# Finishing a quad's last group beside two softmax stages, and splitting the last quad's division over three engines

## The chip, the cores and the metric

The program runs on one core of one Trainium2 chip. The metric is the device time of one execution in microseconds; for the kernel before it is 2020.35 us, the median of three runs (2018.48 to 2020.65). One further execution was profiled and traced. All times of single instructions are from that trace and count from the start of its span.

## What is computed

A graph attention layer with a residual, over 12,500 nodes of 128 features and 200,000 edges that are sorted by their destination:

```python
h = relu(layernorm(x))
hn = (h @ W_node.T).reshape(nodes, 4, 32)
e  = (edge_attr @ W_edge.T).reshape(edges, 4, 32)
att = sum(concat([hn[src], hn[dst], e]) * a, -1)          # one logit per edge and head
att = where(att > 0, att, 0.2 * att)
m   = maximum(segment_max(att, dst), 0)
ex  = exp(att - m[dst])
deg = segment_sum(1, dst)
denom = segment_sum(ex, dst) + (num_edges - deg) * exp(-m)
out = x + segment_sum(ex / denom[dst] * hn[src], dst)
```

The division can wait until the sums are complete, since `denom` belongs to the destination.

## The kernel before

**Tiling.** The edges are cut into 392 *groups* of 511 (and one row that carries a sum over from the group before). Four groups make a *quad*; there are 98 quads, numbered 0 to 97 (`nq` is 98). Two to four quads make a *super*, for which the softmax is done in one go: 28 of them, numbered 0 to 27. Super 2 (the third) holds quads 4 to 7, super 27 (the last) quads 96 and 97. Destinations of a group fit a window of 92 rows.

**The steps of a quad.** `fetch` loads edge features (`ea`), destinations (`db`) and two sets of windows (`pw`, `xw`) through the queue of SyncE (SP), and gathers the source rows from a table in DRAM into `ga`, by sixteen indirect DMAs that GpSimd (POOL) issues one after the other (line 141). `ga` is a ring of eight quads, so a group's gather has to wait until the group 32 places earlier has had its last matmul, line 686. `all_logits` makes the logits: VectorE (DVE) marks the destinations (line 534, which needs `db`), TensorE (PE) multiplies (lines 540, 543), DVE adds the pieces and the gathered part (lines 555, 557). `softmax(s)` turns the logits of a super and scans along the edges; it is one long chain that goes to and fro between DVE, PE and ScalarE (ACT), in five steps separated by `yield` (lines 583 to 592; 595 to 606; 609 to 619; 624 to 641; 644 to 659). `sums(q)` handles the four groups of a quad: DVE weights the gathered rows (line 734) and marks the slots (738), PE multiplies three of four tiles into `acc` (743).

**Completing and dividing.** The first row of a group carries the sum of the group before. So the fourth matmul pair of a group (686) is issued late, by `complete()`, after the next group's first three: DVE scales the carried row (681), ACT copies its count (685), PE multiplies (686), ACT copies `acc` to `pt` (687) and, where a piece of the quad is complete, computes `exp(-m)` into `den` (694). The piece is a whole quad; in quads 95, 96 and 97 it is three, two and one group. The next call of `complete()` divides the piece: six DVE instructions (lines 755, 757, 760, 761, 765, 769), of which the last, adding `x`, is on POOL for quad 96 and for the last group of quad 95. Then SP writes each group's 92 rows (line 772). Windows of neighbouring groups overlap, so each write waits for the one before it.

**Order.** The order of issue on every engine is written out by hand. `together` takes one step of each of its generators in turn. A stage `s` runs the last quad of the super before (`sums(q0 - 1)`), the logits of one quad of the next super and `softmax(s)` side by side. In stage 2 three groups of quad 3, and in stage 27 two groups of quad 95, are issued before that. In both the last group is left incomplete, and its completion and the division come inside the next quad's `sums`, when the softmax is done. In the last two quads the marks of line 738 come from POOL instead (line 711, after the last gather). A few matmuls without use (`run_on`, line 573) keep PE occupied in the last softmax.

Of the kernel before, what the change touches and what calls it, by code (L numbers as in the profile page):

```python
# [8 lines left out]
F32 = mybir.dt.float32  # L9
BF16 = mybir.dt.bfloat16  # L10
I32 = mybir.dt.int32
AF = mybir.ActivationFunctionType
OP = mybir.AluOpType
AX = mybir.AxisListType

P = 128
H, HD = 4, 32
# [7 lines left out]
R_CNT, R_SRC, ROW = H * HW, H * HW + 1, H * HW + 5  # L25
# [5 lines left out]
SPAN = 92  # L31
QG = 4
# [11 lines left out]
def blocks(total, step):  # L44
    return [(i, min(step, total - i)) for i in range(0, total, step)]
# [3 lines left out]
def kernel(  # L49
# [35 lines left out]
    nc = tc.nc  # L85
# [5 lines left out]
    consts = ctx.enter_context(tc.tile_pool(name="consts", bufs=1))  # L91
# [9 lines left out]
    part = consts.tile([P, 1], F32, name="part")  # L101
# [2 lines left out]
    lane = consts.tile([P, WIN], F32, name="lane")  # L104
    nc.gpsimd.iota(lane, pattern=[[1, WIN]], base=0, channel_multiplier=0,
                   allow_small_or_imprecise_dtypes=True)
    ones = consts.tile([P, P], F32, name="ones")
    nc.vector.memset(ones, 1.0)

# [12 lines left out]
    quads = blocks(G, QG)  # L122
    nq = len(quads)
# [21 lines left out]
    def held_gather(q, i, rows, width):  # L145

        nc.vector.memset(ga_all[0:1, q % QUADS, i, 0, 0:1], 0.0)
        gather(q, rows, width, i, i + 1)

    def together(*steps):  # L150
        steps = list(steps)
        while steps:
            steps = [st for st in steps if next(st, steps) is not steps]
# [3 lines left out]
    with tc.manual_schedule():  # L157
# [6 lines left out]
        for _ in range(AT_ONCE):  # L164
            q, i = early.pop(0)
# [12 lines left out]
        with tc.tile_pool(name="prep", bufs=1) as prep, tc.tile_pool(  # L178
            name="prep_ps", bufs=1, space=bass.MemoryType.PSUM
# [127 lines left out]
        with tc.tile_pool(name="node", bufs=2) as node, tc.tile_pool(  # L307
            name="node_ps", bufs=2, space=bass.MemoryType.PSUM
        ) as node_ps, tc.tile_pool(name="index", bufs=1) as index, tc.tile_pool(
            name="index_ps", bufs=1, space=bass.MemoryType.PSUM  # L310
# [111 lines left out]
            step, steps = 0, sum(-(-T // 3) for T in sizes) - 9  # L422
# [40 lines left out]
    with tc.tile_pool(name="work", bufs=2) as work, \  # L463
# [20 lines left out]
        def windows(of, size, g, n):  # L484

            return nc.values_load_multi_w_load_instructions(  # L486
                of[0:1, g:g + n], engines=[mybir.EngineType.SP], min_val=0, max_val=(N - 1) * size,
                skip_runtime_bounds_check_because="a destination's row, and that is a node")[1]
# [16 lines left out]
        def fetch(q):  # L505
            if q not in EA:
                fetch_edges(q)
            fetch_windows(q)
            if q not in GATHERED:
                GATHERED.add(q)  # L510
                gather(q, table, ROW, raws(q), quads[q][1])
# [156 lines left out]
        def complete():  # L668

            division = state.pop("division", None)  # L670
            if begun:
                complete_group(*begun.pop())
            if division:
                divide(*division)

        def complete_group(q, i, ga, hot, pt, acc, fc):
            g0, m = quads[q]
            g = g0 + i
            if g:
                before = state["before"]  # L680
                nc.vector.tensor_tensor(  # L681
                    ga[0:1, i, 0, 0:H * HW].rearrange("p (h w) -> p h w", w=HW),
                    before[WIN:WIN + 1, 0:H * HW].rearrange("p (h w) -> p h w", w=HW),
                    fc.unsqueeze(2).to_broadcast([1, H, HW]), op=OP.mult)
                nc.scalar.copy(ga[0:1, i, 0, R_CNT:R_CNT + 1], before[WIN:WIN + 1, R_CNT:R_CNT + 1])  # L685
            nc.tensor.matmul(acc, hot[:, i, 0, :], ga[:, i, 0, :], start=False, stop=True)  # L686
            nc.scalar.copy(pt[:, i, :], acc)  # L687
            state["before"] = acc

            part = {nq - 1: 1, nq - 2: 2, nq - 3: 3}.get(q, QG)  # L690
            if (i + 1) % part == 0 or i == m - 1:
                lo = i - i % part
                den = work.tile([SPAN, QG, H], F32, name="den")
                nc.scalar.activation(den[:, lo:i + 1, :], pt[0:SPAN, lo:i + 1, R_SRC:R_SRC + H],
                                     AF.Exp, scale=-1.0)
                state["division"] = q, pt, den, lo, i + 1


# [49 lines left out]
        def divide(q, pt, den, lo, hi):  # L748

            n = hi - lo  # L750
            xw = XW[q][:, lo:hi]
            pt = pt[0:SPAN, lo:hi]
            den = den[:, lo:hi]
            others = work.tile([SPAN, QG], F32, name="others")
            nc.vector.tensor_scalar(others[:, :n], pt[:, :, R_CNT], -1.0, float(E),
                                    op0=OP.mult, op1=OP.add)
            nc.vector.tensor_tensor(den, den, others[:, :n].unsqueeze(2).to_broadcast([SPAN, n, H]),
                                    op=OP.mult)
            val = pt[:, :, 0:H * HW].rearrange("p g (h w) -> p g h w", w=HW)
            nc.vector.tensor_tensor(den, den, val[:, :, :, HD], op=OP.add)  # L760
            nc.vector.reciprocal(share_ps[:, :n, :], den)
            if not lo:
                RES[q] = work.tile([SPAN, QG, D], F32, name="res")
            res = RES[q][:, lo:hi]
            nc.vector.tensor_tensor(  # L765
                res[:, :n, :].rearrange("p g (h d) -> p g h d", d=HD), val[:, :, :, 0:HD],
                share_ps[:, :n, :].unsqueeze(3).to_broadcast([SPAN, n, H, HD]), op=OP.mult)
            add = nc.gpsimd if q == nq - 2 or q == nq - 3 and lo else nc.vector
            add.tensor_tensor(res[:, :n, :], res[:, :n, :], xw, op=OP.add)  # L769
            at = windows(base_row, 4 * D, quads[q][0] + lo, n)  # L770
            for i in range(n):
                nc.sync.dma_start(rows_at(out, at[i], 4 * D), as_bytes(res[:, i, :]))
# [14 lines left out]
        def late(q, copy=nc.scalar.copy):  # L787

            return [converted(q, acc_pool, work, copy)]

        def normed(q):
            return several(2, raw_statistics(raw_pool, q), raw_scaled(q))
# [39 lines left out]
        with tc.manual_schedule():  # L832
            for q in range(min(2, nq)):
                fetch(q)
            on_vector = nc.vector.tensor_copy
            assert supers[0] == (0, 2) and supers[1] == (2, 2)

            held = [(q, i) for q in range(raw, min(QUADS, nq)) for i in range(raws(q), quads[q][1])]
            GATHERED.update(range(raw, QUADS))

            def some(*numbers):
                for n in numbers:
                    for _ in range(min(n, len(held))):
                        held_gather(*held.pop(0), table, ROW)
                    yield

            together(some(2, 0, 1, 0, 1), *late(0, on_vector), normed(1))
            together(some(1, 0, 1, 0, 1), *late(1, on_vector), all_logits(0), normed(2))
            together(some(0, 0, 1), all_logits(1), raw_statistics(raw_pool, 3))
            check_steps = checked()  # L850
            for s, (q0, m) in enumerate(supers):


                ahead = list(range(q0 + m, sum(supers[s + 1]))) if s + 1 < len(supers) else []
                now, ahead = ahead[:1], ahead[1:]
                beside = [sums(q0 - 1)] if s else late(2) + [raw_scaled(3)]
                beside += late(raw) if s == 1 else []
                if s in (2, len(supers) - 1):

                    for _ in range(3 if s == 2 else 2):  # L860
                        next(beside[0])
                if not s:
                    beside.insert(0, some(1, 1, 1, 1, 1, len(held)))
                together(*beside, *map(all_logits, now), softmax(s))
                assert not held
                for k in range(m - 1):
                    now, ahead = ahead[:1], ahead[1:]
                    together(sums(q0 + k), *map(all_logits, now), *([] if s else [normed(raw)]))
                    if s > 4:
                        next(check_steps, None)  # L870
                for a in ahead:
                    together(all_logits(a))
                if not s:
                    complete()
                    together(*late(3))
            flush()
            together(check_steps)
            last_sums = sums(nq - 1)
            next(last_sums)
            redo = nc.values_load(flag[0:1, 0:1], min_val=0, max_val=1)  # L880
            together(last_sums)
            complete()
            complete()
# [197 lines left out]
```

## Time and profile before

| | us |
|---|---|
| median of three runs | 2020.35 |
| the profiled execution, its own time | 2020.54 |
| its span, first to last instruction | 2018.7 |
| PE matmul busy | 1376.0 (68%) |
| DVE busy | 1367.8 (68%) |
| ACT busy | 405.9 (20%) |
| POOL busy | 1507.4 (75%) |
| gathers from the table, line 141: 1494 of 949 ns | 1418.3 |
| granted TensorE clock, mean | 0.541 |

Busy shares are means over the whole span. A line of the timeline gives the start, the duration, the engine, the line of the kernel, the operation with its tiles and shapes, how many instructions were merged, and in brackets how long the engine had been idle and what released it. For a DMA queue the duration is that of issuing, with the waits in between.

### The profile page before, as it was taken

To read this page: it belongs to the slowest core of one execution; us is meant where nothing else is said; L and a number is where in the kernel's file an instruction comes from. 1 tells how busy PE (TensorE), PEld (TensorE's weight loads), DVE (VectorE), ACT (ScalarE), POOL (GpSimd) and SP (SyncE) were. 2 spreads that over 40 slices of the span, in tenths; PEclk is the share of its full clock that TensorE was granted. 3 is DMA by queue.
4 is the path that set the end of the run, shared out by engine and by line. 5 is a ranking of instruction groups with operands and counts; after the bars stand their busy time and mean duration, and the time that the engine had idled before them with its cause. 6 is when DMAs were issued, how large, how long until landed. Compare 5 with 4: busy or idle time off the path is not lost.

```text
span 2018.7 us, 27303 instructions
## 1 busy us (share of the span) xinstructions
PE 1376.0 (68%) x7317; PEld 1249.1 (62%) x7317; DVE 1367.8 (68%) x3368; ACT 405.9 (20%) x1532; POOL 1507.4 (75%) x1609
## 2 busy tenths in 40 slices
PE   6687777767767766666757666667566666777776
PEld 4576666667666655656656565556565565666665
DVE  7676766767776765666757656666567576768876
ACT  6664111111111111111111111111111111112112
POOL 7777677777777777777777777777777777777774
PEclk8767555555555555555555555555555555556556
DMA  7665665666656665655555565556555655565640
GB/s 250 211 164 126 156 164 136 157 156 157 151 145 167 154 148 145 157 140 147 146 138 152 134 152 133 151 141 146 137 150 131 155 141 141 135 157 129 155 106 25
DMA packets 195661, 297.23 MB, mean 147 GB/s; under 512 B 70441, under 2 KB 143337, under 8 KB 186098
## 3 DMA queue, kind: packets, MB, share of 16 engines
q1 hardware_dynamic: 143696, 183.27, 34.3%
q0 software_dynamic: 50112, 109.61, 23.3%
q10 hardware_dynamic: 1698, 2.58, 0.4%
q8 instruction: 61, 1.00, 0.2%
q14 instruction: 94, 0.77, 0.1%
HBM read 269.61 MB, written 25.71 MB: 146 GB/s over the span
## 4 chain that ended last, share of the span: by engine, by line
DMA 31%; DVE 22%; PE 16%; POOL 13%; issue 10%; SPq 4%; ACT 4%; DVEq 0%; ACTq 0%; POOLq 0%
POOL ga L141 13%; DMA out_dram<-res 10%; DMA ga<-table,srci 10%; DMA db<-in_dst_dram 9%; PE acc L743 6%; DVE at L534 4%; PE lg L543 3%; DMA pw<-side 2%; DVE ga L734 2%; DVE hot L738 2%; DVE res L765 2%; DVE res L769 2%; PE acc L686 2%; DVE ga L681 1%; SPq L486 1%
## 5 line engine op out<-in xcount | busy, mean ns | idle before, releaser
L141 POOL DMA_INDIRECT ga<-table,srci x1494 | 1418.3, 949 | 460.5 <-issue 394.7
L743 PE MATMUL acc<-ga,hot 128*97 128x137 f32 x2352 | 644.8, 445 | 63.0 <-DVE hot L738 31.0
L743 PEld LDWEIGHTS acc<-ga,hot 128*97 128x97 f32 x2352 | 515.6, 278 | 85.7 <-DVE hot L738 36.9
L540 PEld LDWEIGHTS <-at 92*128 92x128 bf16 x1568 | 214.5, 165 | 506.4 <-DVE at L534 488.0
L540 PE MATMUL lg<-pw,at 92*128 92x12 bf16 x1568 | 169.3, 181 | 435.3 <-DVE at L534 427.3
L543 PE MATMUL lg<-wblk,ea 128*128 128x8 f32 x1568 | 406.8, 357 | 0.0
L543 PEld LDWEIGHTS lg<-wblk,ea 128*128 128x128 f32 x1568 | 379.4, 307 | 0.0
L534 DVE TENSOR_TENSOR at<-const_ps,db 92x512 bf16<-92x512 f32 x392 | 266.9, 682 | 7.7 <-DMA db<-in_dst_dram 1.7
L734 DVE TENSOR_TENSOR ga<-ga,ex_ps 128x528 f32<-128x528 f32 x392 | 268.5, 685 | 0.4
L686 PE MATMUL acc<-ga,hot 128*97 128x137 f32 x784 | 257.2, 431 | 1.3 <-ACT ga L685 1.0
L687 ACT COPY pt<-acc 97x137 f32<-97x137 f32 x392 | 107.4, 274 | 721.9 <-PE acc L686 721.9
L557 DVE TENSOR_TENSOR U<-st,ga 128x64 f32<-128x64 f32 x98 | 26.5, 270 | 308.6 <-DMA ga<-table,srci 300.4
L738 DVE TENSOR_TENSOR hot<-const_ps,slot 128x384 f32<-128x384 f32 x384 | 208.8, 544 | 0.0
L686 PEld LDWEIGHTS acc<-ga,hot 128*97 128x97 f32 x784 | 198.5, 282 | 2.8 <-ACT ga L685 2.8
L681 DVE TENSOR_TENSOR ga<-acc,facs 1x132 f32<-1x132 f32 x391 | 115.7, 296 | 115.0 <-ACT pt L687 107.3
L685 ACT COPY ga<-acc 1x1 f32<-1x1 f32 x391 | 59.9, 153 | 483.0 <-DVE ga L681 476.1
L765 DVE TENSOR_TENSOR res<-pt,const_ps 92x512 f32<-92x512 f32 (+2 forms) x103 | 67.7, 657 | 82.2 <-DMA out_dram<-res 79.0
L141 POOL DMA_INDIRECT ga<-in_x_dram,srci x72 | 69.4, 964 | 23.2 <-issue 18.0
L769 DVE TENSOR_TENSOR res<-res,xw 92x512 f32<-92x512 f32 (+1 forms) x100 | 67.5, 675 | 3.5
L395 PE MATMUL row_ps<-wcat,hT 128*128 128x137 f32 x198 | 39.3, 348 | 21.0 <-DVE tgt L401 11.0
L555 DVE TENSOR_REDUCE st<-lg 128x64 f32<-128x192 f32 x98 | 35.0, 357 | 25.5 <-PE lg L543 24.4
L644 PE MATMUL ex_ps<-ident,ex 64*128 64x64 f32 (+2 forms) x112 | 18.2, 310 | 49.6 <-ACT ex L633 49.6
(137 smaller groups left out, 1032.6 us busy)
## 6 DMA issues: line engine op xcount, KB each, us to landing
db<-in_dst_dram SPq DMA_DIRECT2D x98, 768.0 KB
ea<-in_edge_t_dram SPq DMA_DIRECT2D x98, 512.0 KB
ga<-table,srci POOLq DMA_INDIRECT x1494
xw<-in_x_dram SPq DMA_DIRECT2D x392, 46.0 KB
out_dram<-res SPq DMA_DIRECT2D x392, 46.0 KB
pw<-side SPq DMA_DIRECT2D x392, 2.2 KB
table<-row SPq DMA_DIRECT2D x9, 616.5 KB
xt<-in_x_dram SPq DMA_DIRECT2D x9, 576.0 KB
```

Source lines behind the costliest of these rows:

```text
L141: nc.gpsimd.indirect_dma_start(out=ga[:, i, j, 0:width], out_offset=None, in_=rows, in_offset=bass.IndirectOffsetOnAxis(ap=srci[:, g0 + i, ...
L534: nc.vector.tensor_tensor(at[:, i, :], node_ps[0:SPAN, g0 + i:g0 + i + 1].to_broadcast([SPAN, GE]), db[0:SPAN, i, :], op=OP.is_equal)
L540: nc.tensor.matmul(lg[:, i, j].rearrange("p k h -> p (k h)"), at[:, i, j * P:(j + 1) * P], sw, start=i + j == 0, stop=False, skip_group_ch ...
L543: nc.tensor.matmul(lg[:, i, 2 * w:2 * w + 2, 0, :], ea[:, i, w, :], wblk, start=False, stop=True, skip_group_check=True)
L681: nc.vector.tensor_tensor(ga[0:1, i, 0, 0:H * HW].rearrange("p (h w) -> p h w", w=HW), before[WIN:WIN + 1, 0:H * HW].rearrange("p (h w) -> ...
L686: nc.tensor.matmul(acc, hot[:, i, 0, :], ga[:, i, 0, :], start=False, stop=True)
L687: nc.scalar.copy(pt[:, i, :], acc)
L734: nc.vector.tensor_tensor(val, val, heads(ex)[:, :, :, g - s0].unsqueeze(3).to_broadcast([P, J, H, HW]), op=OP.mult)
L738: nc.vector.tensor_tensor(hot[:, i, :, 0:WIN], lane_ps.unsqueeze(1).to_broadcast([P, J, WIN]), slot[:, g, :].unsqueeze(2).to_broadcast([P, ...
L743: nc.tensor.matmul(acc, hot[:, i, j, :], ga[:, i, j, :], start=j == 1, stop=False)
L765: nc.vector.tensor_tensor(res[:, :n, :].rearrange("p g (h d) -> p g h d", d=HD), val[:, :, :, 0:HD], share_ps[:, :n, :].unsqueeze(3).to_br ...
L769: add.tensor_tensor(res[:, :n, :], res[:, :n, :], xw, op=OP.add)
```

## The change

Two things change. First, in stages 2 and 27 two groups (instead of three in stage 2) are issued ahead, and the rest of that quad's `sums` is wrapped in `finished`, which goes on for two more steps beside the softmax: one that completes the quad's last group and divides what was due (in stage 27 the first three groups of quad 95), and one that divides what is left. Second, in the last quad, number 97, the factor `E - count` and its product with `den` are computed by ACT (an `Identity` activation with a bias tile and a scaled `Copy`) where DVE did it with lines 755 and 757; and the adding of `x` goes to POOL for the first three groups of quad 97, while the last group of quad 95 gets its adding back on DVE.

```diff
+    edges = consts.tile([P, 1], F32, name="edges")
+    nc.vector.memset(edges, float(E))
...
+        def finished(steps):
+            yield from steps
+            complete()
+            yield
+            complete()
...
                 nc.scalar.activation(den[:, lo:i + 1, :], pt[0:SPAN, lo:i + 1, R_SRC:R_SRC + H],
                                      AF.Exp, scale=-1.0)
+                if part == 1:
+                    others = work.tile([SPAN, QG], F32, name="others")
+                    nc.scalar.activation(others[:, 0:1], pt[0:SPAN, i, R_CNT:R_CNT + 1],
+                                         AF.Identity, bias=edges[0:SPAN], scale=-1.0)
+                    nc.scalar.activation(den[:, i, :], den[:, i, :], AF.Copy, scale=others[:, 0:1])
                 state["division"] = q, pt, den, lo, i + 1
...
-            others = work.tile([SPAN, QG], F32, name="others")
-            nc.vector.tensor_scalar(others[:, :n], pt[:, :, R_CNT], -1.0, float(E),
-                                    op0=OP.mult, op1=OP.add)
-            nc.vector.tensor_tensor(den, den, others[:, :n].unsqueeze(2).to_broadcast([SPAN, n, H]),
-                                    op=OP.mult)
+            if q < nq - 1:
+                others = work.tile([SPAN, QG], F32, name="others")
+                nc.vector.tensor_scalar(others[:, :n], pt[:, :, R_CNT], -1.0, float(E),
+                                        op0=OP.mult, op1=OP.add)
+                nc.vector.tensor_tensor(
+                    den, den, others[:, :n].unsqueeze(2).to_broadcast([SPAN, n, H]), op=OP.mult)
...
-            add = nc.gpsimd if q == nq - 2 or q == nq - 3 and lo else nc.vector
+            on_pool = q == nq - 2 or q == nq - 1 and hi < quads[q][1]
+            add = nc.gpsimd if on_pool else nc.vector
...
                 if s in (2, len(supers) - 1):
-                    for _ in range(3 if s == 2 else 2):
+                    for _ in range(2):
                         next(beside[0])
+                    beside[0] = finished(beside[0])
```

## The prediction

> **What bounds the kernel now.** I read the page first, then the stretches of 50 us, then the timelines of the two places where the change acts. In the page's list of groups POOL's gathers stand on top:
>
> ```profile
> L141 POOL DMA_INDIRECT ga<-table,srci x1494 | 1418.3, 949 | 460.5 <-issue 394.7
> ```
>
> 949 ns of work and 0.30 us of issue make 1.25 us per gather, and 1494 of those are 1867 us of a span of 2018.7. The stretches say where POOL does not keep that pace (40 gathers, 37.8 us busy in 50):
>
> ```profile
> 150.00:200.00 50.00, 38.58 (x238) 34.51 (x236) 31.84 (x79) 21.79 (x62) 38.10 (x40) 0.70 0.55 134
> 200.00:250.00 50.00, 36.68 (x214) 33.76 (x214) 36.36 (x83) 7.22 (x29) 34.16 (x36) 0.50 0.62 148
> 250.00:300.00 50.00, 36.67 (x198) 34.14 (x196) 33.68 (x75) 7.39 (x34) 38.00 (x40) 0.53 0.68 168
> ```
>
> Columns are PE, PEld, DVE, ACT, POOL, then clock and DMA. Only 200 to 250 falls short, by four gathers. POOL's timeline shows one pause there, and it is the only one up to the last gather, which ends at 1973.01:
>
> ```profile
> 239.02 0.94 POOL L141 DMA_INDIRECT ga<-table,srci  x1 [0.30 <-issue]
> 244.95 0.94 POOL L141 DMA_INDIRECT ga<-table,srci  x1 [4.98 <-PE acc L686]
> ```
>
> This is the first gather of group 3 of quad 11. Its ring slot is that of group 3 of quad 3, whose matmul 686 ran at 244.01 to 244.67, because it was left for after softmax 2. So the time is: pace of POOL, this pause (4.98 less the usual 0.30, 4.68 us), and the 45.6 us behind the last gather. DVE around the pause:
>
> ```profile
> 227.31 0.69 DVE L534 TENSOR_TENSOR at<-const_ps,db 92x512 bf16<-92x512 f32 x1 [0.45 <-DMA db<-in_dst_dram]
> 230.74 0.69 DVE L595 TENSOR_TENSOR t_ps<-t_ps,low 64x511 f32<-64x511 f32 x1 [1.53 <-ACT low L592]
> 234.01 0.26 DVE L616 TENSOR_TENSOR into<-ends,cont 1x64 f32<-1x64 f32 x1
> 234.81 0.14 DVE L624 COPY col<-ex_ps 64x1 f32<-64x1 f32 x1
> 239.97 0.64 DVE L734 TENSOR_TENSOR ga<-ga,ex_ps 128x528 f32<-128x528 f32 x1
> ```
>
> To be seen: the logits of quad 8 wait for their destinations until 227.31, and the softmax has one hole, 1.53 us. At the end:
>
> ```profile
> 1985.70 0.15 DVE L624 COPY col<-ex_ps 32x1 f32<-32x1 f32 x1 [0.35 <-PE ex_ps L619]
> 2000.51 0.72 POOL L769 TENSOR_TENSOR res<-res,xw 92x256 f32<-92x256 f32 x1 [3.42 <-DVE res L765]
> 2004.52 0.72 POOL L769 TENSOR_TENSOR res<-res,xw 92x256 f32<-92x256 f32 x1 [3.29 <-DVE res L765]
> 2005.27 10.17 SPq L772 DMA_DIRECT2D out_dram<-res  x6
> ```
>
> The last six writes follow each other on SP, 1.98 us apart from first to last (9.89 over five), from the moment that groups 2 and 3 of quad 96 are divided. That moment sets the end; quad 97's data are there before their turn.
>
> **The change part by part: stage 2.** Before, all four groups of quad 3 stood ahead of the softmax. Now the third is followed by the logits of quad 8. DVE is there at about 224.4 (line 681 of 223.37, then 555 and 557, 0.75 us) and waits for `db` until the same 227.31, since SP's order up to that load is unchanged: the 1.9 us of group 3's work no longer fill that wait. Group 3's lines 734, 738 and 681 (0.62, 0.57 and 0.33 from start to start) come after line 583 and fill the 1.53 us hole: line 595 stays at 230.74. Then two things are new on the softmax's chain. Ahead of line 609 line 681 of group 3, 0.33. Ahead of line 624 the whole division of quad 3, as it took from 245.34 to 247.65: 2.31 us. PE's order gives 0.04 us more. Line 624 comes at 234.81 + 2.68 = 237.49, and so does everything up to line 743 of quad 4's group 0: 242.53 + 2.68 = 245.21.
>
> Matmul 686 of quad 3's last group needs lines 681 and 685 and lands near 234.2, ahead of 240.27 when POOL wants the slot: the pause goes. But the next slot, of group 0 of quad 4, is wanted 5.0 us later, at 245.27. Before, matmul 686 of that group ended at 247.60, 5.07 after line 743 of 242.53, and the gather came at 250.11. In those 5.07 stood the 686 of quad 3, 0.46 from start to start, now gone. It ends at 245.21 + 4.60 = 249.81, and POOL goes on at 250.08. The pause has moved by one group, and 0.03 us of it is saved: **0.0 us**, from +1.0 (all 681s and PE passes a little later than counted) to −1.0.
>
> After that the next releases have 2 to 3 us in hand (group 1 at 252.8 for 255.1). The four writes of quad 3 now stand ahead of the loads of quad 11 on SP instead of behind them. They took 268.99 to 276.4, so `db` of quad 11, issued at 258.70, is issued some 7.5 us later, and line 534 of quad 11 (270.39) waits until about 276.5. In exchange the division of quad 5, which waited at line 765 until 278.20 for these writes, does not wait. Quad 14's gathers had 11 to 16 us in hand; 0.
>
> **Stage 27.** Ahead of line 609 come line 681 (0.33) and the division of three groups (1991.83 to 1993.76: 1.93), less the 0.36 that line 611 waited, 1.90. Ahead of line 624 comes the division of one group with its add on DVE (1995.41 to 1996.48 and 0.32: 1.39), less the waits there, some 0.55: line 624 comes 2.75 later, at 1988.45. The idle matmuls, 3.8 us, follow line 619 and so begin and end about 1.9 later; PE then stands idle for some 1.5 us before lines 644 to 654. At the low clock those and their copies took 0.5 us more (1955.07 to 1958.67, against 1989.22 to 1992.32); I take 0.4. Line 743 of quad 96: 1992.84 + 3.15 = 1996.0.
>
> In exchange 3.3 us of DVE work have left quad 96. There PE and the carried row limit: two sets of line 743 at the low clock (1.25 each, from start to start), 686 and 687 (0.95), 681 to 687 of the next group (1.4), 681, the division and POOL's add (0.33, 1.3, 0.75): with what lies between, 7.35 us to the end of the first add, against 8.4 before (1992.84 to 2001.23). The add of groups 2 and 3 ends at about 2007.2 for 2005.24: **+1.9 us**. Bounds: +0.9, if PE has the full clock in quad 96 (six passes 0.72 instead of 1.25, twice), and +2.9, if it stays low throughout.
>
> [...]
>
> **The last quad.** DVE loses lines 755 and 757 (0.26 + 0.19 from start to start) and three adds (0.3). ACT gains two instructions per group that no row shows; the nearest are line 685, 0.15, and line 694 at 92x4, 0.21: 0.15 to 0.25 each, 0.21 taken. They delay line 685 of the next group by about 0.35. The last data come at about 2013.8 (before 2013.28). Their turn on SP is at about 2017, so both gain and loss are covered by up to 3 us: 0. The memset of `edges` is one small DVE instruction at the start: 0.
>
> **Sum**: 2020.54 + 0.0 + 1.9 = 2022.4 for the profiled execution. It lies 0.19 over the median, so **2022.2 us**.
>
> **The rivals.** *The pause goes for good* (faster): the softmax is delayed by next to nothing. It needs line 743 of quad 4 to start at about 240.7, ahead even of its old place; half of that is easier. In full: 4.7 less, 2017.5; half 2019.8. Against it: the division stands in the chain, and the hole is spent on group 3.
>
> *The pause grows* (slower): each us by which softmax 2 is later than 2.7 is a us of POOL, and nothing behind gives it back, since POOL then has no pauses until 1973. It decides above 2024.4 from a delay of 4.9 on, for instance if the division at line 765 waits for a write of quad 1, as quad 5's did for 4.7 us: 2020.35 + 1.9 + 4.7 = 2027; with half of it 2024.6. Against it: those writes ended before 220.
>
> *ScalarE reloads its tables* (slower): if `Identity` is not in the table set of `Exp`, each group of quad 97 has two loads. The trace shows 1.283 us per load, four in all, none after 163.4. Seven on the path, 9.0 us, less 3 covered: 2028. [...]
>
> *Stage 27 costs nothing*: DVE's relief in quad 96 is worth as much as the delay. 2020.3.
>
> **How the numbers follow.** My forecast 0.60 (2021.2 to 2023.4); pause smaller or gone 0.17, of which 0.04 with a cheap end, under 2016.3; pause larger 0.12; tables 0.03; stage 27 free 0.08. Within 0.2% is 4.0 us here, about what a measurement tells from no change. Faster 0.05, same 0.81, slower 0.14 (0.11 of the larger pause and the tables). The range, 2017.5 to 2024.6, leaves out both tails, some 0.16.
>
> **What would show it.** No pause at quad 11's group 3, but one of 4 to 5 us at the next gather; line 624 of stage 2 about 3.1 us behind line 616, where it was 0.8; 35 to 36 gathers in 200 to 250 still. Line 609 of stage 27 some 2.2 us behind the scan of line 599; six last writes starting 1.9 us later against the last gather; no table load in quad 97. Wrong it would be by a full 40 gathers in 200 to 250, or by an end shorter than 45.6 us behind the last gather.

## The result, and the profile after

The changed kernel takes 2022.53 us (median of 22 runs, 2021.07 to 2024.85), the kernel before 2019.45 us (median of 22 runs, 2014.34 to 2023.28). The ratio is 1.0017, 95% interval 1.0010 to 1.0023: a loss of some 3.4 us by the ratio and 3.1 by the medians, smaller than the 0.2% that the prediction named as what a measurement tells from no change. The profiled execution took 2024.38 us, its span is 2022.6 us, and the mean granted clock 0.540.

**Stage 2.** The group of gathers, and the stretch from 200 to 250, whose columns are length, then PE, PEld, DVE, ACT and POOL with their instructions, clock, DMA share and GB/s:

```profile
L143 POOL DMA_INDIRECT ga<-table,srci x1494 | 1418.5, 949 | 460.8 <-issue 390.6
```

```profile
200.00:250.00 50.00, 34.56 (x215) 32.14 (x215) 36.72 (x83) 7.07 (x28) 34.94 (x38) 0.57 0.66 161
```

The cost of a gather and the idle time before gathers (460.8 for 460.5) are what they were, and the stretch still falls short of 40 gathers. POOL's timeline around the pause, and DVE's:

```profile
239.14 0.94 POOL L143 DMA_INDIRECT ga<-table,srci  x1 [0.30 <-issue]
...
242.88 0.94 POOL L143 DMA_INDIRECT ga<-table,srci  x1 [0.30 <-issue]
247.91 0.94 POOL L143 DMA_INDIRECT ga<-table,srci  x1 [4.09 <-PE acc L695]
```

```profile
225.16 0.69 DVE L536 TENSOR_TENSOR at<-const_ps,db 92x512 bf16<-92x512 f32 x1 [1.94 <-DMA db<-in_dst_dram]
...
232.32 0.26 DVE L618 TENSOR_TENSOR into<-ends,cont 1x64 f32<-1x64 f32 x1
...
235.39 0.14 DVE L626 COPY col<-ex_ps 64x1 f32<-64x1 f32 x1
240.49 0.64 DVE L748 TENSOR_TENSOR ga<-ga,ex_ps 128x528 f32<-128x528 f32 x1
```

The gather at 239.14 is that of quad 11's group 3, where POOL had stood for 4.98 us: it no longer waits. Four gathers on, at group 0 of quad 12, POOL stands for 4.09 us for matmul 695 of quad 4's first group. Line 626 (624 before) is 3.07 us behind line 618, where it was 0.80 behind. The pause has moved by one group. The last gather ends at 1972.80 (1973.01 before).

**The end.** SP's last six writes, POOL's adds of `x`, and POOL's closing instructions (minimum, median and maximum in ns, then the first and the last start):

```profile
2007.22 10.99 SPq L788 DMA_DIRECT2D out_dram<-res  x6
```

```profile
2002.47 0.72 POOL L785 TENSOR_TENSOR res<-res,xw 92x256 f32<-92x256 f32 x1 [12.26 <-DVE res L780]
2006.47 0.72 POOL L785 TENSOR_TENSOR res<-res,xw 92x256 f32<-92x256 f32 x1 [3.29 <-DVE res L780]
2008.14 0.45 POOL L785 TENSOR_TENSOR res<-res,xw 92x128 f32<-92x128 f32 x1 [0.95 <-DVE res L780]
...
2012.65 0.45 POOL L785 TENSOR_TENSOR res<-res,xw 92x128 f32<-92x128 f32 x1 [2.07 <-DVE res L780]
```

```profile
L902 POOLq INC_SWDGE_SEM  x1: 1831/1831/1831, 2013.1 to 2013.1; - x1
```

```profile
L1094 POOLq DRAIN  x3: 40/107/6774, 2015.0 to 2022.3; - x3
```

After its last instruction POOL raises a semaphore (INC_SWDGE_SEM, 1.83 us) and drains its queue (the longest DRAIN, 6.77 us); here that lasts from 2013.1 to 2021.8, and the span ends at 2022.6. Before, POOL's last instruction was the add at 2004.52, and the same closing work was over at 2013.6, long before the last write:

```profile
L1077 POOLq DRAIN  x3: 40/107/6774, 2006.9 to 2018.4; - x3
```

Counted from the end of the last gather, in us, where the closing drain's end is its 6.77 us alone:

| | six last writes start | last write issued | POOL's drain ends | span ends |
|---|---|---|---|---|
| before | 32.26 | 42.15 | 40.62 | 45.65 |
| after | 34.42 | 45.13 | 48.96 | 49.79 |
| difference | +2.16 | +2.98 | +8.34 | +4.14 |

The 4.14 us have three parts. 2.16 come from the start of the writes, as the prediction has it. 0.82 come from the writes themselves, nearly all of it from one that took 2.97 us, from its start to that of the next, instead of some 2.2. The remaining 1.16 are POOL's drain: from the last write to the end of the span there were 3.50 us before, and 4.66 now.

**ScalarE's two instructions**, for one group of quad 97:

```profile
2011.23 0.28 ACT L707 ACTIVATE others<-pt,edges 92x1 f32<-92x1 f32 x1
2011.54 0.30 ACT L709 ACTIVATE den<-den,others 92x4 f32<-92x4 f32 x1
```

They cost 0.28 and 0.30 us, and there is no table load in quad 97: the last of the four in this profile starts at 162.39.

### The profile page after: what moved, and what is told of

Same layout as the page of the kernel before. It is cut to its first block, busy times and chain, and to the rows that moved or that the text cites. A ratio compares the mean times of both kernels' runs of the same rounds, so it can differ in the third digit from the quotient of the medians.

```text
span 2022.6 us, 27306 instructions
## 1 busy us (share of the span) xinstructions
PE 1374.0 (68%) x7317; PEld 1246.9 (62%) x7317; DVE 1367.7 (68%) x3359; ACT 408.2 (20%) x1540; POOL 1508.1 (75%) x1611
## 5 line engine op out<-in xcount | busy, mean ns | idle before, releaser
L143 POOL DMA_INDIRECT ga<-table,srci x1494 | 1418.5, 949 | 460.8 <-issue 390.6
L397 PE MATMUL row_ps<-wcat,hT 128*128 128x137 f32 x198 | 36.3, 328 | 22.7 <-DVE tgt L403 10.6
```

The source lines that it names most:

```text
L143: nc.gpsimd.indirect_dma_start(out=ga[:, i, j, 0:width], out_offset=None, in_=rows, in_offset=bass.IndirectOffsetOnAxis(ap=srci[:, g0 + i, ...
```

## The experiments

The theory after the result: the change has three separable parts. Stage 2 only moves the pause. Stage 27 puts two divisions into the softmax's chain, which the end pays for. The last quad's adds on POOL put POOL's closing work at the end. The main rival: the loss comes from one place alone, the softmax of stage 27, and the rest is chance.

**One part alone: stage 2.**

```diff
-                    for _ in range(3 if s == 2 else 2):
+                    for _ in range(2):
                         next(beside[0])
+                    if s == 2:
+                        beside[0] = finished(beside[0])
```

> Stage 2's part alone: two groups ahead, then quad 3's last group completed and divided beside softmax 2; stage 27 and the last quad as before. Theory (the pause only moves): no pause at quad 11's group 3, one of 4 to 5 us at the next gather, quad 12's group 0; the last gather ends within 1 us of 1973.0, and the time is within 1.5 us of the kernel before. Rival (stage 2 gains what the pause was worth and the end loses more than it shows): last gather at about 1968.5, time 4 us below before.

Measured: 2021.01 us for 2021.44 of before on that chip, ratio 0.9997 (0.9986 to 1.0008). DVE and POOL:

```profile
226.31 0.69 DVE L534 TENSOR_TENSOR at<-const_ps,db 92x512 bf16<-92x512 f32 x1 [2.91 <-DMA db<-in_dst_dram]
...
236.81 0.14 DVE L624 COPY col<-ex_ps 64x1 f32<-64x1 f32 x1
```

```profile
249.34 0.94 POOL L141 DMA_INDIRECT ga<-table,srci  x1 [5.34 <-PE acc L693]
```

The pause is at group 0 of quad 12, 5.34 us long, and the time is unchanged within its interval. The pause and the end of the last gather, 1974.40, lie somewhat outside what was expected (4 to 5 us, and 1973.0 within 1 us); the table below shows where that comes from.

**One part alone: stage 27.** The last group of quad 95 has its add on DVE, as in the changed kernel.

```diff
+                    if s > 2:
+                        beside[0] = finished(beside[0])
```

> Stage 27's part alone: quad 95 completed and divided beside softmax 27, its last add on DVE; the last quad's division as before. Theory (the division stands in the softmax's chain): from the last gather's end to the first of the six last writes 34.4 us, where it was 32.3, and the span's end about 48 us behind the last gather; the pause of stage 2 as before; time 2 to 3 us above before. Rival (the end is lost in the last quad): 32.3 and 45.6, time as before.

Measured: 2024.38 us, ratio 1.0018 (1.0008 to 1.0029). The six last writes start 34.43 us behind the last gather, the span ends at 47.87: both as expected. This part alone is as slow as the whole change.

**One part alone: the last quad.** The division's first two steps on ACT and the adds of quad 97 on POOL, with the order of before.

```diff
-            add = nc.gpsimd if q == nq - 2 or q == nq - 3 and lo else nc.vector
+            on_pool = q == nq - 2 or q == nq - 3 and lo or q == nq - 1 and hi < quads[q][1]
+            add = nc.gpsimd if on_pool else nc.vector
```

> The last quad's division alone: two steps on ACT, three adds on POOL; no completing beside a softmax. Theory (POOL's closing work, 8.6 us behind its last instruction, becomes the end): the six writes start as before, 32.3 us behind the last gather; POOL's last add ends some 38.5 us behind it, the closing drain some 47.1, and the span some 47.8 instead of 45.6: time 2 us above before. Rival (hidden behind the six writes): 45.6, time as before. Third: DVE's relief tells, time 1 us below.

Measured: 2023.68 us, ratio 1.0013 (0.9999 to 1.0026). The writes start at 31.91, the last is issued at 41.61, and POOL's drain ends at 45.71, the span at 46.54. POOL's last add and its drain:

```profile
2011.23 0.45 POOL L785 TENSOR_TENSOR res<-res,xw 92x128 f32<-92x128 f32 x1 [1.32 <-DVE res L780]
```

```profile
L1093 POOLq DRAIN  x3: 40/107/6774, 2013.6 to 2020.9; - x3
```

The drain sets the end: with the 3.50 us that otherwise follow the last write the span would have ended at 45.1, so the adds cost 1.4 us in this profile. I had expected more (47.8), since the last add came 1.5 us earlier than I had it.

**The last quad without POOL.** The former kernel with the adds of quad 97 on DVE, as before; the two instructions stay on ACT.

```diff
-            on_pool = q == nq - 2 or q == nq - 3 and lo or q == nq - 1 and hi < quads[q][1]
+            on_pool = q == nq - 2 or q == nq - 3 and lo
```

> The last quad's division alone, with the two steps on ACT but all of quad 97's adds on DVE: third experiment without POOL. Theory (in that experiment POOL's closing work set the end): the drain ends some 40.6 us behind the last gather as before, the span some 45.1 to 45.6; time as before within 1 us. Rival (ACT's longer chain sets the end): last write's issue later than before's 42.2 us behind the last gather, and the span 46.5 as in the third.

Measured: 2020.12 us for 2019.85, ratio 1.0004 (0.9993 to 1.0014). POOL's drain ends at 39.68, ahead of the last write at 42.16. So ACT's part shows no cost. That the former run is slower because of the adds is read from the place of the drain in the two profiles; the two ratios, 1.0013 and 1.0004, have intervals that overlap.

**The whole change with those adds on DVE.**

```diff
-            on_pool = q == nq - 2 or q == nq - 1 and hi < quads[q][1]
+            on_pool = q == nq - 2
```

> The changed kernel with quad 97's three adds back on DVE; POOL's last instruction is then quad 96's second add. Theory (POOL's closing work ended the changed kernel): the closing drain ends long before SP, the span ends some 3.5 us behind the last write's issue, 48.6 us behind the last gather instead of 49.8: time 1 to 1.5 us below the changed kernel, some 2 above before. Rival (the closing work was covered by the writes): time as the changed kernel.

Measured: 2023.28 us for 2021.44, ratio 1.0016 (1.0005 to 1.0027). In its profile the drain ends at 42.22 and the span at 47.09 instead of 49.79, with the writes starting at 33.85:

```profile
L1094 POOLq DRAIN  x3: 40/107/6774, 2005.1 to 2016.5; - x3
```

The trace says that the drain is off the end. The ratio beside the changed kernel's own, 1.0016 against 1.0017, does not show the 1.2 us; the intervals are wider than that.

**Quad 3's last group completed beside the softmax, its division left in quad 4.** Three groups are issued ahead, as before the change. If the division is what delays the chain of stage 2, this must shorten the pause; if the completion is, it must not.

```diff
+        def completed(steps):
+            yield from steps
+            due.append(state.pop("division", None))
+            complete_group(*begun.pop())
+            due.append(state.pop("division"))
...
+                    if s == 2:
+                        beside[0] = completed(beside[0])
```

> The kernel before with one part of stage 2's change: three groups ahead as before, quad 3's last group completed beside softmax 2, but its division left where it was, in quad 4's second step. Theory (the division in the softmax's chain is what moved the pause): matmul 686 of that group ends near 232, line 624 stays within 0.5 us of its old distance, and of the pause some 2.3 us are left at quad 12's group 0: last gather 2 to 3 us earlier, time 2 to 3 us below before. Rival (the completion itself delays the softmax): a pause of 4 to 5 us at quad 12's group 0, time as before.

Measured: 2018.32 us for 2019.85, ratio 0.9994 (0.9983 to 1.0004). POOL does not pause at all, where 2.3 us of pause were expected, and the stretch is full:

```profile
228.28 0.68 DVE L534 TENSOR_TENSOR at<-const_ps,db 92x512 bf16<-92x512 f32 x1
...
235.90 0.14 DVE L624 COPY col<-ex_ps 64x1 f32<-64x1 f32 x1
```

```profile
200.00:250.00 50.00, 37.87 (x225) 34.40 (x224) 39.15 (x88) 7.50 (x30) 37.75 (x40) 0.53 0.62 147
```

**The same, and in stage 2 each step of the softmax issued ahead of the logits of quad 8.**

```diff
-                together(*beside, *map(all_logits, now), softmax(s))
+                together(*beside, *([softmax(s), all_logits(now[0])] if s == 2 else [*map(all_logits, now), softmax(s)]))
```

> As the one before, and in stage 2 each step of the softmax is issued ahead of that step's logits of quad 8. Theory (softmax 2 stands behind the wait for the destinations of quad 8, and each earlier us of it is a us less of pause): softmax 2 some 2 us earlier, a pause under 1 us is left, time 3.5 to 4.5 us below before. Rival (the pause's rest hangs on something else, such as the logits of quad 8 that now come late): 2 us or more of pause left.

Measured: 2017.90 us for 2019.85, ratio 0.9993 (0.9984 to 1.0002). The column comes 5.21 us behind the first line 534 of quad 8 instead of 7.61, and a rest of the pause is left, as expected. The time, expected 3.5 to 4.5 us below before, is 1.4 us below it by the ratio, within the interval:

```profile
225.48 0.69 DVE L534 TENSOR_TENSOR at<-const_ps,db 92x512 bf16<-92x512 f32 x1 [0.67 <-DMA db<-in_dst_dram]
...
230.69 0.14 DVE L624 COPY col<-ex_ps 64x1 f32<-64x1 f32 x1
```

```profile
245.37 0.94 POOL L141 DMA_INDIRECT ga<-table,srci  x1 [1.06 <-PE acc L696]
```

These runs show what makes the length of the pause. From the gather of quad 10's group 3 to that of quad 12's group 0 there are 25.0 us when POOL does not pause; the starts that lie between are, in us:

| | gather 10.3 to first line 534 of quad 8 | to line 624 | to gather 12.0 | sum |
|---|---|---|---|---|
| before | 7.02 | 7.50 | 15.30 | 29.82 |
| stage 27 alone | 5.72 | 7.64 | 15.28 | 28.64 |
| last quad alone | 6.58 | 7.47 | 15.30 | 29.35 |
| last quad without POOL | 6.45 | 7.46 | 15.30 | 29.21 |
| quad 95's completion only (below) | 4.14 | 7.46 | 15.29 | 26.89 |
| after | 6.01 | 10.23 | 12.53 | 28.77 |
| stage 2 alone | 6.97 | 10.50 | 12.53 | 30.00 |
| after, adds on DVE | 4.73 | 10.25 | 12.53 | 27.51 |
| quad 3's completion only | 4.48 | 7.61 | 12.89 | 24.98 |
| and softmax first | 5.83 | 5.21 | 14.68 | 25.72 |

The last two columns of steps together are 22.8 to 22.9 in the old order of stage 2, and 22.8 to 23.0 in the new one: the 2.7 to 3.0 us by which the softmax is late are made up behind it, in two ways. The last matmul of quad 4's group 0, on which gather 12.0 waits, ends 12.25 us behind the column instead of 12.79, since the completion of quad 3 no longer stands before it. Before and after:

```profile
246.93 0.66 PE L686 MATMUL acc<-ga,hot 128*97 128x137 f32 x2
```

```profile
246.98 0.66 PE L695 MATMUL acc<-ga,hot 128*97 128x137 f32 x2
```

And in the old order POOL had not stood waiting for this matmul at all: released for group 3 of quad 11, it started there 10.14 us behind the column and reached gather 12.0 four gathers later, at its own pace, at 15.30. In the new order it starts gather 12.0 as soon as the matmul is done, at 12.53. That the two ways together match the delay is a matter of these sizes, not a rule.

The first column, which ends with the landing of `db` of quad 8 wherever the line names what released it, alone makes the pauses of kernels with one order differ. It also explains why quad 3's completion only has no pause: `db` came after 4.48 us there. The matmul for gather 12.0 ends 12.33 us behind the column in that kernel, so the two steps could take 20.2 us, and with the 7.02 us of the kernel before some 2.2 us over the 25.0 would be left, which is what was expected. With the softmax first the two steps take 19.9.

**Quad 95's last group completed beside softmax 27, the divisions left in quad 96.**

```diff
+                    if s > 2:
+                        beside[0] = completed(beside[0])
```

> The kernel before with one part of stage 27's change: quad 95's last group completed beside softmax 27, its two divisions left in quad 96. Theory (the divisions in the softmax's chain are what the end pays): line 624 at most 0.4 us later than before, the six last writes start within 0.5 us of 32.3 behind the last gather, the span ends at 45.2 to 45.9; time as before within 1 us. Rival (the idle matmuls' place and the clock are what it pays): the same as with the divisions only if line 619 is late, which it is not, so 34 would speak for neither.

Measured: 2019.54 us for 2019.85, ratio 1.0000 (0.9991 to 1.0010). The six writes start at 32.29 and the span ends at 45.46, as before the change. The column comes 3.03 us behind the scan of line 599, where it was 3.00. So the completion costs nothing at the end, and the 2 us of stage 27 are the two divisions (one of which has its add on DVE there).

**Softmax first in three of four steps; and twelve idle matmuls instead of eight beside stage 27's divisions.** In the kernel with the softmax first, the logits of the fourth step stood on PE ahead of the softmax's transposes and waited there for DVE's marks: the transposes (line 644) begin 6.88 us behind the column, where they begin 4.19 behind it with quad 3's completion only. The first of these two kernels puts that step back. The second takes the kernel with stage 27 alone and gives `run_on` 12 for 8, to see whether PE's clock is what kept quad 96 from being faster.

```diff
+        def in_turn(soft, logs):
+            for k in range(QG):
+                for st in (soft, logs) if k < QG - 1 else (logs, soft):
+                    next(st)
+                yield
+            together(logs, soft)
```

```diff
-                run_on(8)
+                run_on(12)
```

> As the kernel with the softmax ahead of the logits in stage 2, but in the fourth step the logits of quad 8 go first again, since their matmuls stood in front of the softmax's transposes and cost it some 2 us there. Theory (the pause is the lateness of line 743 of quad 4): that line another 1.5 us earlier, no pause over 0.4 us left at quad 11 or 12; time 3.5 to 5 us below before with what a whole pause was worth there (4 to 5 us), and the median some 2 to 3 below, since the pause of the old order varies. Rival (earlier loads, not the softmax, set POOL's pace there): the pause back at another gather, time within 1 us of before.

> Stage 27's part alone with twelve idle matmuls instead of eight in the last softmax. [...]

> The kernel of the former run with the softmax step ahead of the logits of quad 8 in the first three steps and behind them in the fourth, once more, to be set beside runs in which the time before is about 2020 us. Quad 3's last group is completed beside softmax 2, its division is left in quad 4's second step. Theory (the pause belongs to the chain softmax 2, scaled rows of quad 4, last matmul of group 0 of quad 4; every us by which that chain is earlier is a us of POOL's stream): the wanted time of the gather of quad 12's group 0 is met or missed by less than 0.5 us, so the gathers from group 10.3 to group 12.0 take 25 to 25.6 us instead of 26.9 to 29.8, and the time is 0.10 to 0.2% under before (about 2 to 4 us). Rival (what POOL gains there is lost again before the end): the pause goes but the ratio stays within 0.05% of 1.

> Stage 27 with the divisions beside the softmax and twelve instead of eight idle matmuls, to be set beside runs in which the time before is about 2020 us. [...] Rival C: the longer row of idle matmuls delays the last passes of the softmax on PE, column to first add grows, and the writes start at 34.8 or later.

Measured: the chips that these two pairs ran on took 2561.27 and 2579.15 us for the kernel before, so the times cannot be set beside the others. There POOL is not bound by its own pace. The same stretch length in the kernel before (on a usual chip) and in the first of these (on a slower one) has 40 and 32 gathers:

```profile
800.00:850.00 50.00, 36.21 (x190) 32.87 (x191) 38.49 (x91) 8.09 (x33) 37.89 (x40) 0.50 0.57 144
```

```profile
1000.00:1050.00 50.00, 28.18 (x147) 24.94 (x146) 30.10 (x70) 6.97 (x28) 30.50 (x32) 0.50 0.50 129
```

POOL's pauses there are some 3 us long and come after about every twelve gathers: 2.80 us before the gather at 1013.92 and 3.00 before the one at 1031.76, with twelve gathers from the one to the other. For 102 and 101 of POOL's waits in the second pair of profiles, 270.5 and 260.3 us in all, the trace says `remote` and names no instruction of the program. Relative to before on the same chip the softmax-first kernel is 0.9965 (0.9947 to 0.9984) and 0.9966 (0.9949 to 0.9982), that is 0.34% faster on both. Its pauses at the two gathers in question add up to 13.0 and 13.7 us there, against 17.7 in both runs of the other kernel, which has the old order in stage 2: some 4 to 5 of the 9 us. Where the others come from was not found. What was expected of the time and of the pause on a usual chip was not tested by these runs.

For the idle matmuls the ratios are 0.9996 (0.9981 to 1.0012) and 1.0022 (1.0006 to 1.0038): no gain. But what lies between line 624 of stage 27 and the last six writes can be compared, since by then no gather is left but those long done. The windows run from the one to the other; the last three columns are granted clock, DMA share and GB/s, for before, after, stage 2 alone, and the run with twelve idle matmuls that had the better clock:

```profile
1985.70:2005.30 19.60, 14.26 (x77) 11.94 (x78) 15.66 (x43) 5.27 (x22) 6.16 (x12) 0.81 0.05 15
```

```profile
1987.70:2007.20 19.50, 13.90 (x72) 11.71 (x72) 12.61 (x32) 5.12 (x21) 3.95 (x8) 0.72 0.05 13
```

```profile
1986.10:2007.60 21.50, 16.78 (x77) 14.62 (x78) 15.63 (x43) 5.27 (x22) 7.16 (x14) 0.62 0.05 14
```

```profile
2542.30:2559.80 17.50, 13.17 (x80) 11.20 (x80) 12.73 (x32) 4.63 (x19) 1.45 (x2) 0.85 0.05 14
```

And for the softmax first and quad 95's completion only, which had nearly the same clock:

```profile
1979.70:2000.20 20.50, 14.03 (x77) 11.64 (x78) 15.59 (x43) 5.26 (x22) 7.31 (x14) 0.75 0.05 14
```

```profile
1981.60:2001.20 19.60, 13.96 (x75) 11.79 (x76) 15.27 (x42) 4.68 (x20) 6.12 (x12) 0.74 0.05 15
```

| order of stage 27 | stretches of full clock, us behind line 624 | line 624 to the writes |
|---|---|---|
| old: stage 2 alone | from 16.2 on | 21.49 |
| old: softmax first | to 1.4, from 11.5 | 20.55 |
| old: softmax first in three of four, two runs | to 4.9, from 11.7; to 5.2, from 12.1 | 20.53, 20.47 |
| old: last quad without POOL | 3.4 to 6.8, 10.2 to 17.1 | 19.82 |
| old: last quad alone | 3.8 to 7.2, from 10.6 | 19.72 |
| old: quad 3's completion only | 4.1 to 7.5, from 10.9 | 19.72 |
| old: before | 4.0 to 7.4, from 10.8 | 19.57 |
| quad 95's completion only | to 1.1, from 11.3 | 19.57 |
| new: after; stage 27 alone | from 11.0 | 19.53; 19.52 |
| new: after, adds on DVE | 2.8 to 6.2, from 9.6 | 18.69 |
| new: twelve idle matmuls, first run | 4.3 to 7.7, 11.2 to 14.6, from 18.0 | 19.68 |
| new: twelve idle matmuls, second run | 5.1 to 18.7 | 17.47 |

With the full clock from 11 to 12 us on, the old order takes 20.5 and the new one 19.5. But quad 95's completion only, which leaves both divisions in quad 96, also takes 19.57. So the 1.0 us comes with the completion: its two matmuls of line 686 no longer stand at the head of quad 96 (9.05 us behind line 624 with the softmax first). That DVE is relieved of the divisions in quad 96 shows no gain beside that. The kernel with the completion only is a single profile. With the full clock from 5 us on the new order takes 17.5, so that quad 96 is not bound by DVE whatever the clock. Twelve idle matmuls gave that in one profile and not in the other, so the number of them does not settle the clock.

## Why the prediction was right

**Stage 2, 0.0 us: right, and by the mechanism.** The softmax's column was to come 2.68 us later; against the first line 534 it came 2.73 (after) to 3.00 us later (stage 2 alone). The division was to be 2.31 of that and is 2.27 (3.07 for 0.80 between lines 618 and 626). Line 748 of quad 4 and all behind it were to follow by as much, and the last matmul of quad 4's group 0 was to gain 0.46 on the column, for the completion that had stood before it: it gained 0.54. That the pause reads 4.09 instead of 4.98 comes from the wait for `db`, which ended 1.0 us earlier against the gathers in this profile. It need not be an effect of the change: other runs of the old order have the same wait from 4.1 to 7.0 us. The prediction took the landing of `db` for fixed. It isn't, and it spread the pause by more than the prediction's ±1.0 (1.77 to 4.98 us in the old order). The rival of a larger pause and that of a vanishing one both fail in the table: the sum of the two steps is the same in both orders to 0.3 us. Of what was to follow, the division of quad 5 no longer waits, as foreseen, and line 534 of quad 11 waits for its load until 271.04, not until 276.5; no pause of POOL hangs on it.

**Stage 27, +1.9 us: right in size, its parts less so.** The prediction's own terms, 3.15 later and 1.05 back, make 2.1; it wrote 1.9. The writes start 2.16 us later in the profiles; over the profiles on usual chips 32.3 in the mean of seven with the divisions in quad 96 (31.3 to 33.2), and 34.2 in the mean of three with the new order (33.9 to 34.4), which is +1.96. In the pair of before and after two misses cancel, and that is luck. The delay of line 626 against the scan of stage 27 is 3.18 us for the 2.75 predicted (6.18 for 3.00). Against the last gather it is 2.20, because the scan itself came 0.98 us earlier; it starts anywhere from 8.7 to 10.2 us behind the last gather in those seven. From the column to line 743 of quad 96 there are 7.50 us for 7.14, at a clock of 0.50 against 0.72: 0.36 us, for 0.4 predicted. From there to the end of the first add the prediction gave back 1.05, and the profile gives back 0.39 (8.00 for 8.39), at a clock of 0.72 against 0.81 from the column to the writes. At nearly equal clock the 1.05 is about right, 1.0 by the table. It comes from where the prediction's list has it, PE and the carried row, which lose the completion, and not from the 3.3 us of DVE work that left quad 96.

The prediction's sum takes line 743's first two sets in quad 96 at the low clock, 1.25 us each, and that held: after the change the clock is 0.50 until 1998.66, and these sets run from 1995.19 to 1998.22. That it would hold was the author's estimate; what opens the full clock no run shows. Before, PE was busy for 3.14 of the 3.42 us ahead of 1989.66, at a clock of 0.50, and the full clock was granted from there to 1993.07, and again from 1996.48 to 2006.72; after the change it was granted from 1998.66 to 2008.90. Why two runs of one kernel with the same twelve idle matmuls get 17.47 and 19.68 was not found. After the change the idle matmuls come later, and no full clock opens before 11.0. But stage 2 alone has its idle matmuls where they were before, up to 3.3 us behind line 624, and none opens before 16.2 there, so the displacement is not shown to be the reason.

**The last quad, 0: the step that failed.** The prediction looked at when the data are ready for SP and found 3 us of cover for it, which is right: the writes follow each other as before. It did not follow POOL to its last instruction. Moving three adds to POOL moved its last instruction from 2004.52 to 2012.65, and behind it come 1.83 and 6.77 us of closing work that the trace of before showed in full. This made 1.16 us of the 4.14 in the profile, and 1.4 in the run with the last quad alone; with the adds back on DVE the drain is off the end again. In the medians this is not resolved. ACT's two instructions at 0.28 and 0.30 us were taken at 0.21, within bounds of 0.15 to 0.25 that were too tight; the last quad without POOL shows that it doesn't matter. The rival of table loads fell: both profiles have the same four loads of 1.283 us, the last at 163.36 before and at 162.39 after, and beside the `Identity` of quad 97 there is none. That the loads were unlikely was the author's estimate, since no run before had an `Identity`.

**The sum.** 2022.2 us was forecast and 2022.53 measured, but part of that agreement is luck. The forecast started from 2020.35 us, and beside the changed kernel the kernel before took 2019.45. The forecast loss is 1.9 us and the measured one 3.1 to 3.4; the 1.16 us of POOL's drain, which the prediction left out, is of the size of what is missing, but no time here resolves it. The parts alone do not add up to the whole either: stage 27's, +3.6 us by its ratio, the last quad's, +2.6, and stage 2's, −0.6, make 5.6, where the whole change costs 3.4; each of these is uncertain by some 1 to 3 us. What is shown is that stage 27's divisions cost time, that its completion and ACT's part show no cost, and that stage 2 shows neither gain nor loss.

**A better version.** Completing without dividing in stage 2 took the pause away in one profile, in part because `db` came early, and with the softmax first 0.76 us of it were left. The times, 0.06 and 0.07% under before, are not beyond their intervals, and the 2 to 4.5 us that were expected of them were not found. On the two slower chips softmax first in three of four steps is 0.34% faster than before, beyond its interval. No version was shown to be faster on a usual chip.

## What to carry to other kernels

Work that is moved ahead of a dependent chain in order to fill a hole has to be split by what others wait for: here the completion released a buffer and was free, while the division, for which nobody waited, put its 2.3 us into the chain, so that the wait only moved to the next buffer. Before an engine is given a part of the last work, follow it to its very last instruction and add the time that it takes to close down, 8.6 us for POOL here, which was hidden as long as POOL finished early. Where a pause begins with a transfer's landing, look at several runs before reading a microsecond of difference in it as an effect of the change: here the landing came 4.1 to 7.0 us behind one and the same gather in kernels of one order.

## What the runs showed of the hardware

POOL's closing work took 8.6 us (1.83 and 6.77 us, the same to the nanosecond in the profiles of before, after, stage 2 alone, stage 27 alone, the last quad alone, the adds on DVE and the second run with twelve idle matmuls). It began 0.5 us behind the start of POOL's last add, at 2005.0 before and 2013.1 after. The wait for one 768 KB load, seen from the gathers, ranged from 4.1 to 7.0 us in kernels with the same order, and with it the pause. Of the last six writes of 46 KB, one took 2.97 us after the change, from its start to that of the next, where the others of before and after took 1.75 to 2.25. And the kernel before took about 2020 us on most chips of these runs and 2561 and 2579 us on two others, where POOL's gathers took 950 and 953 ns each in the second pair of profiles, for 949 before, but paused some 3 us after about every twelve (2.80 and 3.00 us in the softmax-first kernel, at 1013.92 and 1031.76); why those chips do so stays open.
